# Attention of a hybrid transformer block: the order in which first-pass and second-pass score tiles take three PSUM buffers

## The chip, the cores and the metric

The kernel runs on one core of a Trainium2 chip. Its engines work side by side, each through its own instructions in order: TensorE (PE in the profile, with its weight loads as PEld), VectorE (DVE), ScalarE (ACT), GpSimd (POOL), and SyncE (SP), which issues most DMAs. The metric is the device time of one execution in microseconds; lower is better.

## The reference

The block takes x of shape (4, 1024, 256) in float32 and applies four residual steps, each on a layer-normed x: causal attention with 16 heads of 16 channels, a feed-forward step with one of four experts per token, a Mamba-2 step, and the feed-forward step again.

```python
x = x + attention(layernorm(x))   # LoRA-adapted Wq, Wk, Wv, Wo; rotary q and k
x = x + ffn(layernorm(x))         # top-1 of 4 experts, silu(x Wg) * (x Wu), then Wd
x = x + x' + mamba2(x')           # x' = layernorm(x)
x = x + ffn(layernorm(x))
```

Inside attention, which is all that this change touches:

```python
Q, K = rope(Q), rope(K)
scores = einsum('bhqd,bhkd->bhqk', Q, K) / sqrt(16)
attn = softmax(where(causal, scores, -inf))
out = einsum('bhqk,bhkd->bhqd', attn, V)
```

## The kernel before, in words

The program is laid out by a framework that tracks tiles: a Python program traces instructions in some order, a scheduler orders each engine's instructions with regard to that order, and semaphores are put where an engine needs another's result or a buffer that is still in use. An engine's own order is fixed once the program is built.

Attention works on groups of four heads. There are 16 groups in all (4 batches of 4 groups), and the code calls each group a head, `heads[n]`. For one of them the softmax takes two passes over the scores, since the row maximum is needed first:

- The **first pass**, `maxima` (L723 to L742), computes scores with queries on the partitions. For a query block `qb` of 128 and a half `h` of the keys, and for each pair `p` of two heads, two matmuls fill a tile `s1` of 128 x 2 x 512 (L733; one matmul for each head `a` of the pair, on 64 rows of the array). DVE adds the causal mask on the diagonal block (L741) and reduces the row maximum (L742). There are 12 units (`first_pass`).
- `negated` (L744 to L761) turns the maxima into a row of negated maxima, `mneg`, by four transposes. It runs after unit 3 of the first pass and after its last.
- The **second pass**, `exps` (L763 to L786), computes scores with keys on the partitions. For a block of keys `kc` and a half `qt` of the queries, and for each pair `p`, four matmuls fill a tile `s2` of the same size (L771): two with k and q, two that add the negated maximum through a selection matrix. ACT exponentiates it into a tile `pe` in SBUF (L779), and POOL zeroes what is above the diagonal (L782). There are 12 units (`second_pass`), of 512, 384, 256 or 128 columns a head.
- `weigh` (L788 to L801) multiplies `pe` with v into an accumulator `acc` (L793): four matmuls, each on 32 columns of the array. Float32 operands make each of these two instructions in the profile, so a unit has eight. `weigh` of a unit is traced one unit later, through the variable `late`.

Both `s1` and `s2` come from `ps2`, one ring of three buffers of two PSUM banks each (tag "two"; FFN tiles take `gu` from the same ring). A new tile takes the buffer of the tile three places earlier in traced order, when that has been read.

The loop at L889 goes through the heads, and for each through the 12 units of the second pass. In a unit it traces, in this order: the first-pass unit of the next head (`look(after, u)`, pairs 0 and 1), the second-pass unit of this head (`H.exps`, pairs 0 and 1), the weighing of the previous unit, and a piece of the head after the next (`then.piece(u)`): in units 2, 3, 6 and 7 `project` (L653), with matmuls L660, copies on ACT (L667, L672), the rotation on POOL (L675 to L683), casts on ACT (L690) and subtractions on POOL (L693); in units 4, 5, 8 and 9 `turn` (L697), four transposes (L701) and a copy on ACT (L708). Then come pieces of other work: the loading and output projection of batches, the routing of tokens, and FFN tiles. Head 0's own first pass stands before the loop.

After attention, the FFN, the Mamba step and the second FFN follow, from about 1273 us on.

Of the kernel before, what the change touches and what calls it, by code (L numbers as in the profile page):

```python
# [64 lines left out]
def bcast(ap, axis, n):  # L65

    a = ap.unsqueeze(axis)
    shape = list(a.shape)
    shape[axis] = n
    return a.to_broadcast(shape)  # L70
# [3 lines left out]
def hybrid_block(ctx: ExitStack, tc: tile.TileContext, t, out: bass.AP):  # L74
    nc = tc.nc
# [9 lines left out]
    def ps2(name):  # L85
        return psum_now["pool"].tile([P, 2, 512], F32, tag="two", name=name, bufs=psum_now["two"])
# [415 lines left out]
    def attention(pa):  # L502
# [34 lines left out]
        sels = []  # L537
        for p in range(2):
            w = pa.tile([P, P], F32, tag="sel", name=f"sel_{p}", bufs=2)
# [3 lines left out]
            r = pa.tile([P, P], F32R, tag="sel_r", name=f"sel_r_{p}", bufs=2)  # L543
# [96 lines left out]
        class Heads:  # L640
# [79 lines left out]
                    for p in range(2):  # L720
                        self.turn(1, u - 12, p)

            def maxima(self, qb, h):  # L723

                if self.mx is None:
                    self.mx = pa.tile([P, NBLK, 4, 2], F32, tag="mx", name=f"mx_{self.name}", bufs=2)
                keys = (qb + 1) * P
                w = min(512, keys - 512 * h)
                for p in range(2):
                    sc = ps2(f"s1_{self.name}_{qb}_{h}_{p}")  # L730
                    for a in range(2):
                        r = slice(64 * a, 64 * a + 64)
                        nc.tensor.matmul(  # L733
                            sc[:, a, 0:w],
                            self.q[p, qb // 4][r, qb % 4 * P : (qb % 4 + 1) * P],
                            self.k[p, h][r, 0:w],
                            start=True,
                            stop=True,
                        )
                    if 512 * h + w == keys:  # L740
                        nc.vector.tensor_tensor(sc[:, :, w - P : w], sc[:, :, w - P : w], bcast(amats, 1, 2), ALU.add)  # L741
                    nc.vector.tensor_reduce(self.mx[:, qb, 2 * p : 2 * p + 2, h], sc[:, :, 0:w], axis=AX.X, op=ALU.max)  # L742

            def negated(self, qt):  # L744

# [14 lines left out]
                self.mneg[qt] = pa.tile([P, 512], F32R, tag="mneg", name=f"mneg_{self.name}_{qt}", bufs=3)  # L760
                nc.vector.tensor_copy(self.mneg[qt], pt)  # L761

            def exps(self, qt, kc):  # L763
                off = max(0, kc * P - qt * 512)
                pes = []
                for p in range(2):
                    sc = ps2(f"s2_{self.name}_{qt}_{kc}_{p}")
                    for part in range(2):
                        for a in range(2):
                            r = slice(64 * a, 64 * a + 64)  # L770
                            nc.tensor.matmul(  # L771
                                sc[:, a, off:512],
                                sels[p][r, :] if part else self.k[p, kc // 4][r, kc % 4 * P : (kc % 4 + 1) * P],
                                self.mneg[qt][r, off:512] if part else self.q[p, qt][r, off:512],
                                start=(part == 0),
                                stop=(part == 1),
                            )
                    pe = pa.tile([P, 2, 512], F32, tag="pe", name=f"pe_{self.name}_{qt}_{kc}_{p}", bufs=4)
                    nc.scalar.activation(pe[:, :, off:512], sc[:, :, off:512], AF.Exp, scale=1.0 / math.sqrt(DK))  # L779
                    if kc >= 4 * qt:  # L780
                        diag = pe[:, :, off : off + P]
                        nc.gpsimd.affine_select(  # L782
                            diag, diag, [[0, 2], [1, P]], ALU.is_ge, 0.0, base=0, channel_multiplier=-1
                        )
                    pes.append(pe)
                return off, pes  # L786

            def weigh(self, qt, kc, off, pes):  # L788
                nkc = 4 * (qt + 1)
# [45 lines left out]
        second_pass = [(qt, kc) for qt in range(2) for kc in range(4 * (qt + 1))]  # L835
        heads = [Heads(n) for n in range(NB * HG)]

        def look(H, u):
            qb, h = first_pass[u]
            H.maxima(qb, h)  # L840
            if (qb, h) == (3, 0):
                H.negated(0)
            if u == len(first_pass) - 1:
                H.negated(1)
# [8 lines left out]
        H, after = heads[0], heads[1]  # L853
# [20 lines left out]
        ]  # L874
        for u in range(len(first_pass)):
            beside[u]()
            look(H, u)
        one_now = ps1
        late = None
        starting, sending, tiles, n_done = iter(()), iter(()), fill(), 0  # L880
# [1 line left out]
        def stage(n_halves):  # L882

            nonlocal n_done
            n_tiles = full_tiles(n_halves * TB) - n_done
            n_done += n_tiles
            return one_by_one(n_tiles, x_mid, f"f1_{n_halves}")

        for n, H in enumerate(heads):  # L889
            after = heads[n + 1] if n + 1 < len(heads) else None  # L890
            then = heads[n + 2] if n + 2 < len(heads) else None
            for u, (qt, kc) in enumerate(second_pass):
                if after:
                    if n and u < 2:
                        after.piece(12 + u)
                    look(after, u)
                off, pes = H.exps(qt, kc)
                if late:
                    late[0].weigh(*late[1:])
                late = (H, qt, kc, off, pes)  # L900
                if then:
                    then.piece(u)
                if H.c == 0 and n and u == 3:
                    sending = finish(H.b - 1, 1)
                if H.c == HG - 1 and u == 7:
                    sending = finish(H.b, 0)
                if H.c == 1 and H.b + 1 < NB and u == 8:
                    starting = begin(H.b + 1)
                next(starting, None)
                next(sending, None)  # L910
                if u not in (2, 3, 6, 7):
                    next(tiles, None)
                if H.c == 0 and n and u == 9:
                    for _ in tiles:
                        pass
                    tiles = stage(2 * H.b)
# [359 lines left out]
    for n, H in enumerate(halves):  # L1276
        after = halves[n + 1] if n + 1 < len(halves) else None
# [90 lines left out]
```

## Time and profile before

| what | us |
| --- | --- |
| median of 3 runs | 2649.07 |
| lowest and highest of them | 2639.3, 2653.35 |
| profiled execution, its own time | 2623.66 |
| its span, first to last instruction | 2622.0 |
| PE busy | 2301.9 |
| DVE busy | 1468.6 |
| POOL busy | 841.8 |
| ACT busy | 804.6 |

The profile is one execution. A line of a group gives the line of the kernel, the engine, the operation, what it writes and reads with the shape, and the count; after the bar the busy time of the group and the mean of one instruction in ns; after the second bar the idle time of the engine ahead of these instructions and who ended most of it. A line of the waits gives who waited for whom, then the total in us, how many times, and the longest. A line of the timeline gives the start, the duration, the engine and what ran; neighbours of one kind are merged. TensorE's matmuls are pipelined and their ends are modelled, so its busy time is not a measure of work: starts are safer.

### The profile page before, as it was taken

What the parts mean: (1) busy time and instruction counts of PE and PEld (TensorE: products, weight loads), DVE (VectorE), ACT (ScalarE), POOL (GpSimd) and SP (SyncE); (2) the same over time, 40 slices, a digit from 0 to 9 for tenths busy, and PEclk for the clock granted to TensorE, in tenths of its full rate; (3) what the DMA queues carried; (4) which work ended last, traced back from release to release, by engine and by line L of the source; (5) the groups of instructions that cost most, each with busy time, mean ns of one, the idle gap of its engine ahead of it and who ended that gap; (6) DMA issues with size and microseconds to landing.
All of it is one profiled execution on the core that took longest, in us unless ns stands there. A gap on an engine that the chain in (4) does not pass through costs nothing.

```text
span 2622.0 us, 32689 instructions
## 1 busy us (share of the span) xinstructions
PE 2301.9 (88%) x11460; PEld 1557.9 (59%) x11460; DVE 1468.6 (56%) x3573; ACT 804.6 (31%) x1582; POOL 841.8 (32%) x1244
## 2 busy tenths in 40 slices
PE   6778989998998999899989978777879899898798
PEld 4434444544555555555678854544757667687687
DVE  5445456555555455554443358777778676754232
ACT  3344444344443333333211114232323222211011
POOL 3323344233342333321222215344343333331121
PEclk8689899998899999899999988787989999999899
DMA  9993012100132111312465410001131321323552
GB/s 217 185 178 80 10 33 77 49 10 7 31 110 78 65 57 36 100 65 72 143 204 173 162 41 0 9 18 44 47 113 37 133 82 60 117 71 104 204 180 66
DMA packets 151205, 227.26 MB, mean 87 GB/s; under 512 B 25595, under 2 KB 113021, under 8 KB 151041
## 3 DMA queue, kind: packets, MB, share of 16 engines
q1 hardware_dynamic: 139328, 194.25, 25.5%
q0 software_dynamic: 11392, 30.52, 3.3%
q8 instruction: 91, 1.49, 0.2%
q14 instruction: 74, 0.60, 0.1%
q10 hardware_dynamic: 320, 0.39, 0.1%
HBM read 162.52 MB, written 62.86 MB: 86 GB/s over the span
## 4 chain that ended last, share of the span: by engine, by line
PE 63%; DVE 16%; POOL 7%; ACT 5%; issue 4%; DMA 4%; SPq 1%; POOLq 0%; ACTq 0%; DVEq 0%
PE gu_f L418 19%; PE y_f L432 9%; PE acc L793 6%; PE s L771 5%; PE mo_m L1239 3%; PE s L733 3%; PE qkv L660 3%; DVE mx L742 2%; PE turn L701 2%; DVE xc_m L1066 2%; PE xbc_m L1053 2%; POOL rope L680 2%; ACT pe L779 2%; PE y_m L1216 2%; PE po L627 1%
## 5 line engine op out<-in xcount | busy, mean ns | idle before, releaser
L742 DVE TENSOR_REDUCE mx<-s 128x2 f32<-128x1024 f32 (+3 forms) x384 | 357.2, 949 | 152.9 <-PE s L733 151.1
L779 ACT ACTIVATE pe<-s 128x1024 f32<-128x1024 f32 (+3 forms) x384 | 303.7, 808 | 297.8 <-PE s L771 293.3
L418 PE MATMUL gu_f<-t_xT_f,t_Wg_f 128*128 128x256 f32 x1216 | 325.4, 388 | 16.3 <-issue 10.2
L418 PE MATMUL gu_f<-t_xT_f,t_Wu_f 128*128 128x256 f32 x1216 | 317.2, 382 | 0.0
L793 PE MATMUL acc<-pe,v 128*32 128x512 f32 (+3 forms) x1536 | 287.7, 525 | 11.6 <-POOL pe L782 8.2
L432 PE MATMUL y_f<-t_Wd_f,t_h_f 128*128 128x256 f32 x1216 | 281.5, 386 | 6.3 <-DVE state_m L1212 2.4
L418 PEld LDWEIGHTS gu_f<-t_xT_f,t_Wg_f 128*128 128x128 f32 x1216 | 229.4, 194 | 59.5 <-issue 17.6
L143 ACT ACTIVATE t_h_f<-gu_f 128x512 f32<-128x512 f32 x152 | 90.6, 596 | 566.5 <-PE gu_f L418 566.5
L432 PEld LDWEIGHTS y_f<-t_Wd_f,t_h_f 128*128 128x128 f32 x1216 | 228.6, 192 | 49.9 <-issue 9.1
L418 PEld LDWEIGHTS gu_f<-t_xT_f,t_Wu_f 128*128 128x128 f32 x1216 | 232.2, 192 | 32.6 <-issue 1.0
L771 PE MATMUL s<-qs,ks 64*128 64x512 f32 (+3 forms) x768 | 187.4, 431 | 45.6 <-DVE mx L742 23.4
L144 DVE SCALAR_TENSOR_TENSOR t_h_f<-t_h_f,gu_f 128x512 f32<-128x512 f32 x152 | 103.9, 683 | 219.4 <-ACT t_h_f L143 219.4
L782 POOL TENSOR_SCALAR_AFFINE_SELECT pe<-pe 128x256 f32<-128x256 f32 x256 | 103.8, 407 | 380.5 <-ACT pe L779 379.4
L741 DVE TENSOR_TENSOR s<-s,amats 128x256 f32<-128x256 f32 x256 | 104.4, 426 | 200.8 <-PE s L733 160.4
L771 PEld LDWEIGHTS s<-qs,ks 64*128 64x128 f32 x768 | 87.2, 195 | 157.9 <-issue 42.4
L733 PE MATMUL s<-ks,qs 64*128 64x512 f32 (+3 forms) x768 | 158.6, 430 | 11.8 <-ACT pe L779 5.3
L771 PE MATMUL s<-mneg,sel_r 64*128 64x512 f32 (+3 forms) x768 | 167.3, 379 | 0.0
L733 PEld LDWEIGHTS s<-ks,qs 64*128 64x128 f32 x768 | 74.7, 198 | 105.9 <-issue 58.6
L675 POOL TENSOR_TENSOR rope<-qk,rope 128x256 f32<-128x256 f32 x62 | 45.2, 729 | 285.0 <-ACT qk L672 285.0
L1066 DVE SCALAR_TENSOR_TENSOR xc_m<-raw_m,conv_w,xc_m 128x512 f32<-128x512 f32 x144 | 119.3, 839 | 0.4
L660 PE MATMUL qkv<-weff,xT 128*128 128x192 f32 x512 | 114.8, 367 | 4.4 <-ACT qk L672 2.2
L660 PEld LDWEIGHTS qkv<-weff,xT 128*128 128x128 f32 x512 | 90.8, 208 | 42.8 <-issue 19.4
(340 smaller groups left out, 3616.7 us busy)
## 6 DMA issues: line engine op xcount, KB each, us to landing
t_Wg_f<-in_Wg SPq DMA_DIRECT2D x38, 1024.0 KB, 7.1
t_Wu_f<-in_Wu SPq DMA_DIRECT2D x38, 1024.0 KB, 8.0
t_Wd_f<-in_Wd SPq DMA_DIRECT2D x38, 1024.0 KB, 5.9
sorted_rows<-blank SPq DMA_DIRECT2D x17, 2056.0 KB, 31.2
t_rows_f<-sorted_rows SPq DMA_DIRECT2D x22, 514.0 KB, 5.7
x<-in_x SPq DMA_DIRECT2D x8, 512.0 KB, 3.9
o<-raw SPq DMA_DIRECT2D x128, 32.0 KB, 2.0
inv<-dens SPq DMA_DIRECT2D x128, 32.0 KB, 2.0
```

What stands on the lines that cost most here:

```text
L144: nc.vector.scalar_tensor_tensor(dst, t, 1.0, src, op0=ALU.add, op1=ALU.mult)
L418: nc.tensor.matmul(gu[:, i, j, :], w[which][:, k, f * P : (f + 1) * P], xT[:, k, :], start=(k == 0), stop=(k == 1))
L432: nc.tensor.matmul(y, hs[f // 2][:, f % 2, i * P : (i + 1) * P], wd[:, f, :], start=(f == 0), stop=(f == DFF // P - 1),)
L660: nc.tensor.matmul(pp[:, i, 0:192], B.xT[:, k, tok], B.weff[:, k, self.c * 192 : (self.c + 1) * 192], start=(k == 0), stop=(k == 1),)
L733: nc.tensor.matmul(sc[:, a, 0:w], self.q[p, qb // 4][r, qb % 4 * P : (qb % 4 + 1) * P], self.k[p, h][r, 0:w], start=True, stop=True,)
L741: nc.vector.tensor_tensor(sc[:, :, w - P : w], sc[:, :, w - P : w], bcast(amats, 1, 2), ALU.add)
L742: nc.vector.tensor_reduce(self.mx[:, qb, 2 * p : 2 * p + 2, h], sc[:, :, 0:w], axis=AX.X, op=ALU.max)
L771: nc.tensor.matmul(sc[:, a, off:512], sels[p][r, :] if part else self.k[p, kc // 4][r, kc % 4 * P : (kc % 4 + 1) * P], self.mneg[qt][r, of ...
L779: nc.scalar.activation(pe[:, :, off:512], sc[:, :, off:512], AF.Exp, scale=1.0 / math.sqrt(DK))
L782: nc.gpsimd.affine_select(diag, diag, [[0, 2], [1, P]], ALU.is_ge, 0.0, base=0, channel_multiplier=-1)
L793: nc.tensor.matmul(self.acc[32 * j : 32 * j + 32, off:512], self.v[:, kc, (DK + 1) * j : (DK + 1) * j + 32], pes[j // 2][:, j % 2, off:512 ...
L1066: nc.vector.scalar_tensor_tensor(acc, raw[:, k : k + TB], conv_w[:, cc, k : k + 1], acc, op0=ALU.mult, op1=ALU.add)
```

## The change

`maxima` and `exps` take the pair `p` as an argument and handle one pair instead of looping over both; `look` passes it on and ends early for pair 0. The loop traces, for each pair, the second-pass tile of this head and then the first-pass tile of the next one. `after.piece(12 + u)` stays ahead of them and `weigh` behind them. The same instructions are issued.

```diff
-            def maxima(self, qb, h):
+            def maxima(self, qb, h, p):
...
-                for p in range(2):
-                    sc = ps2(f"s1_{self.name}_{qb}_{h}_{p}")
...
+                sc = ps2(f"s1_{self.name}_{qb}_{h}_{p}")
...
-            def exps(self, qt, kc):
+            def exps(self, qt, kc, p):
                 off = max(0, kc * P - qt * 512)
-                pes = []
-                for p in range(2):
-                    sc = ps2(f"s2_{self.name}_{qt}_{kc}_{p}")
...
+                sc = ps2(f"s2_{self.name}_{qt}_{kc}_{p}")
...
-                return off, pes
+                return off, pe
...
-        def look(H, u):
+        def look(H, u, p):
             qb, h = first_pass[u]
-            H.maxima(qb, h)
+            H.maxima(qb, h, p)
+            if p == 0:
+                return
             if (qb, h) == (3, 0):
                 H.negated(0)
...
             beside[u]()
-            look(H, u)
+            for p in range(2):
+                look(H, u, p)
...
             for u, (qt, kc) in enumerate(second_pass):
-                if after:
-                    if n and u < 2:
-                        after.piece(12 + u)
-                    look(after, u)
-                off, pes = H.exps(qt, kc)
+                if after and n and u < 2:
+                    after.piece(12 + u)
+
+                pes = []
+                for p in range(2):
+                    off, pe = H.exps(qt, kc, p)
+                    pes.append(pe)
+                    if after:
+                        look(after, u, p)
                 if late:
                     late[0].weigh(*late[1:])
                 late = (H, qt, kc, off, pes)
```

More of the change, by code (lines that the diff above doesn't have):

```diff
@@ L728, in maxima @@
                 w = min(512, keys - 512 * h)
-                for p in range(2):
-                    sc = ps2(f"s1_{self.name}_{qb}_{h}_{p}")
[L731 to L742, printed above, removed]
+                sc = ps2(f"s1_{self.name}_{qb}_{h}_{p}")
+                for a in range(2):
+                    r = slice(64 * a, 64 * a + 64)
+                    nc.tensor.matmul(
+                        sc[:, a, 0:w],
+                        self.q[p, qb // 4][r, qb % 4 * P : (qb % 4 + 1) * P],
+                        self.k[p, h][r, 0:w],
+                        start=True,
+                        stop=True,
+                    )
+                if 512 * h + w == keys:
+                    nc.vector.tensor_tensor(sc[:, :, w - P : w], sc[:, :, w - P : w], bcast(amats, 1, 2), ALU.add)
+                nc.vector.tensor_reduce(self.mx[:, qb, 2 * p : 2 * p + 2, h], sc[:, :, 0:w], axis=AX.X, op=ALU.max)
             def negated(self, qt):
@@ L761, in negated @@
                 nc.vector.tensor_copy(self.mneg[qt], pt)
-            def exps(self, qt, kc):
+            def exps(self, qt, kc, p):
                 off = max(0, kc * P - qt * 512)
-                pes = []
-                for p in range(2):
-                    sc = ps2(f"s2_{self.name}_{qt}_{kc}_{p}")
[L768 to L783, printed above, removed]
-                        )
-                    pes.append(pe)
-                return off, pes
@@ new lines, in exps @@
+                sc = ps2(f"s2_{self.name}_{qt}_{kc}_{p}")
+                for part in range(2):
+                    for a in range(2):
+                        r = slice(64 * a, 64 * a + 64)
+                        nc.tensor.matmul(
+                            sc[:, a, off:512],
+                            sels[p][r, :] if part else self.k[p, kc // 4][r, kc % 4 * P : (kc % 4 + 1) * P],
+                            self.mneg[qt][r, off:512] if part else self.q[p, qt][r, off:512],
+                            start=(part == 0),
+                            stop=(part == 1),
+                        )
@@ L788, in weigh @@
+                pe = pa.tile([P, 2, 512], F32, tag="pe", name=f"pe_{self.name}_{qt}_{kc}_{p}", bufs=4)
+                nc.scalar.activation(pe[:, :, off:512], sc[:, :, off:512], AF.Exp, scale=1.0 / math.sqrt(DK))
+                if kc >= 4 * qt:
+                    diag = pe[:, :, off : off + P]
+                    nc.gpsimd.affine_select(diag, diag, [[0, 2], [1, P]], ALU.is_ge, 0.0, base=0, channel_multiplier=-1)
+                return off, pe
             def weigh(self, qt, kc, off, pes):
```

## The prediction

> **What bounds the kernel now.** I read the page first, then the table of windows for the attention stretch (first to last second-pass matmul, 84 to 1273 us), then the waits of TensorE in that stretch, then the timeline of one unit. From the page:
>
> ```profile
> span 2622.0 us, 32689 instructions
> PE 2301.9 (88%) x11460; PEld 1557.9 (59%) x11460; DVE 1468.6 (56%) x3573; ACT 804.6 (31%) x1582; POOL 841.8 (32%) x1244
> L742 DVE TENSOR_REDUCE mx<-s 128x2 f32<-128x1024 f32 (+3 forms) x384 | 357.2, 949 | 152.9 <-PE s L733 151.1
> L779 ACT ACTIVATE pe<-s 128x1024 f32<-128x1024 f32 (+3 forms) x384 | 303.7, 808 | 297.8 <-PE s L771 293.3
> L793 PE MATMUL acc<-pe,v 128*32 128x512 f32 (+3 forms) x1536 | 287.7, 525 | 11.6 <-POOL pe L782 8.2
> ```
>
> TensorE is the busiest engine, and the two engines that empty the score banks wait for it (the last column). The windows say the same of the attention stretch:
>
> ```profile
> 84.00:1273.00 1189.00, 1075.12 (x6016) 596.05 (x6016) 626.56 (x1465) 488.49 (x934) 391.73 (x767) 0.93 0.26 68
> ```
>
> The columns are length, then busy time of PE, PEld, DVE, ACT and POOL. DVE is busy 53% of this stretch and ACT 41%, so neither is full; PE is idle for 1189 - 1075 = 114 us. Who ends that idle time (total, times, longest):
>
> ```profile
> PE turn L701 <- POOL qtok L693: 25.3, 14, 2.3
> PE s L771 <- DVE mx L742: 23.4, 30, 5.1
> PE s L771 <- ACT pe L779: 17.8, 15, 3.0
> PE acc L793 <- POOL pe L782: 8.2, 5, 2.8
> PE s L733 <- ACT pe L779: 5.3, 13, 1.4
> ```
>
> The second, third and fifth rows, 46.5 us, are waits for one of the three score buffers. The first row is another chain: the turns wait for the rotated q that POOL makes. Busy time hides a further loss, seen in the timeline of one unit (start, duration):
>
> ```profile
> 546.60 0.74 PE L733 MATMUL s<-ks,qs 64*128 64x512 f32 x4
> 547.14 2.35 DVE L742 TENSOR_REDUCE mx<-s 128x2 f32<-128x1024 f32 x2 [5.32 <-PE s L733]
> ...
> 547.73 1.05 PE L793 MATMUL acc<-pe,v 128*32 128x512 f32 x2
> 547.89 1.02 ACT L779 ACTIVATE pe<-s 128x1024 f32<-128x1024 f32 x1 [0.61 <-PE s L771]
> 548.70 0.19 PEld L771 LDWEIGHTS s<-qs,ks 64*128 64x128 f32 x2 [0.84 <-DVE mx L742]
> 548.70 0.50 PE L771 MATMUL s<-qs,ks 64*128 64x512 f32 x2
> ...
> 549.37 1.06 PE L793 MATMUL acc<-pe,v 128*32 128x512 f32 x6
> ```
>
> Two first-pass tiles are filled, then one second-pass tile; the next needs the buffer that DVE is still reducing. A quarter of the weighing (2 of 8 acc matmuls) was ordered into that hole, and the other 6 follow later. Both pieces last about 1 us: 0.97 us from start to start for 2, and the whole of 8 also takes 0.99 us where it is not cut. A cut weighing costs a second full pass.
>
> **What the Trainium skill says.** "TensorEngine Tiling (Array Packing)", Key Properties, says that changing the tiling mode drains TensorE. The trace agrees: two passes of L660 step 0.325 us when another L660 follows and 0.418 when a row-tiled score matmul does, 0.093 us for a change. "TensorE: Matmul & The Clock Gate", The mechanism, says that tiles in different column groups run together, which is why 2 and 8 acc matmuls last alike. "PSUM — Partial Sum Buffer", Engine vs sequencer instructions, says that matmuls start in program order: a score matmul that waits for a bank holds everything behind it, as at 548.70.
>
> **The change part by part.** No instruction is added, removed or resized, and no DMA moves. Call a first-pass tile A and a second-pass tile B. Before, the ring of three buffers is taken A0 A1 B0 B1; after, B0 A0 B1 A1. Head 0's own first pass before the loop, and the last head, which has no A beside it, keep their order.
>
> *Which waits go and come.* Each tile waits for the release three places earlier. Before: B1 waits for this unit's A0 (DVE), the other three for tiles of the unit before. After: A1 waits for this unit's B0 (ACT), B0 and B1 for the previous A0 and A1 (DVE), A0 for the previous B1 (ACT). So in each unit one near wait is exchanged for another. The exponential is the shorter one: 1.02 us at full width, against 1.2 for a reduce with a mask addition of 0.43 ahead of it in 8 of 12 units; and between B0 and A1 lie A0 and a larger B1 (0.23 + 0.46 us) where A1 and B0 lay before.
>
> *TensorE's own work.* The two programs' instruction orders, as built, differ more than the diff tells, since a scheduler places the independent work. Counting unbroken pieces of weighing by width, 512 / 384 / 256 / 128 columns: 161, 56, 54, 52 before, and 159, 47, 46, 37 after. At 0.98, 0.77, 0.58 and 0.36 us a piece (start to start in the trace) that is 2.0 + 6.9 + 4.6 + 5.4 = 19 us less. Changes of tiling mode from the first B to the last acc go from 1130 to 990: 140 x 0.093 = 13 us less. Row pairs of B cut apart rise by 12, at some 0.2 us: 2 us more. Sum: 30 us less work.
>
> *One unit by hand*, from the durations above, with a projection (L660, 1.3 us) and full width: B0 starts at 0, its exponential runs from 0.73 to 1.75 as in the timeline; A0 and B1 are done at 1.15; A1 starts at 1.85, 0.7 us idle; then weighing 1.0, projection 1.3 and three changes of mode, and the next B0 starts at 4.65. Before, the timeline has successive units of this kind at 546.60, 551.85 and 556.98: 5.2 us. With a turn (0.66 us) instead of a projection it comes to 4.0, and to 4.3 if B0's exponential is 0.3 us late behind ACT's casts; the trace has 4.76 to the next unit (561.74). So a full-width unit gains about 0.5 us. Narrow units have shorter drains and shorter pieces: half of that.
>
> *The sum.* 15 heads x 12 units have both passes, half of them near full width: 90 x 0.5 + 90 x 0.25 = 67 us. That is an upper value, because heads that carry FFN tiles, or the ends and starts of batches, have other work to cover waits; there only the 30 us of work counts. I take the middle, 48 us, less the turn rows: PE reaches a turn some 0.2 us earlier against the same POOL chain, 14 times, 3 us back. **Forecast: 45 us less.** The profiled execution took 2623.7 us outside and 2622.0 as span, so it would take 2579; the median of the three timed runs is 25 us above it, and 2649 - 45 = 2604.
>
> *What is costed at nothing.* `negated` now follows the second A behind a B1: its result is used by the next head, for half 0 eight units later and for half 1 four units later; without that cover, its chain would cost the 1 us or so of four transposes and a copy, 32 times. Mask and reduce of one tile now follow each other on DVE where two additions stood together; DVE is idle 47% of the stretch. Weighing comes behind A1 and so may start later, but the weighed tiles are a unit old. On ACT, exponentials now stand between the q/k copy and the casts that wait for POOL's rotation in 41 of 64 projections, 18 before; ACT waits 2.3 us there (125.0 us in 54 waits). That unblocks a release; its own worth lies between 0 and 23 us (23 exponentials a microsecond earlier), and the unit's sum holds it.
>
> **The rivals.** *The rotation takes over.* The turns behind a projection wait for a chain of copy, POOL's three operations (2.4 us), cast and subtraction; if PE saves its time just ahead of them, the first waits row grows from 25 to some 55 us and the 30 us of work come back. For it: that row is the largest, and two projections precede the turn by one and two narrow units. Against: only one place in a head. It leaves about 10 us: 2639.
>
> *Slower: A1 is left bare.* The same-unit wait on ACT has only A0 and B1 as cover, and ACT is in order: an exponential behind casts that wait for POOL can be late by 2.3 us. If the bare wait averages 0.6 us in all 180 units, it costs 108 us; against it stand 30 us of work and the 46.5 us of buffer waits removed. 108 - 77 = 31 us slower, 2680. It decides from 77 / 180 = 0.43 us a unit. My own 0.7 at full width lies above that, which is why this is a serious rival; against it, narrow units need only 0.3, and in 86 places a quarter of the weighing still stands as cover.
>
> *The change does not do what it says*, because the scheduler regroups the tiles: runs of A and of B alternate 722 times in the new order and 360 in the old, so this is out.
>
> **How the numbers follow.** Forecast case (gain of 20 to 90 us) 0.68; rotation takes over 0.15; A1 bare 0.13; something larger than all this, 0.04. The range of the first case is 2560 to 2630; to leave out no more than 2 in 10 it reaches through the second case into the third: 2556 to 2660. A measurement of this kernel tells about 0.5% (13 us) from no change: faster by more 0.70, within 0.14, slower by more 0.16.
>
> **What would show it.** In the new profile, PE's waits on DVE's reduce should fall under 12 us and its score waits should be on ACT, at the first pass line. The attention stretch should end near 1225 to 1235 us instead of 1273, the rest staying at 1349. Acc matmuls should come mostly in eights. If PE's first-pass matmuls wait over 70 us on ACT the slower rival holds; if the turns wait over 45 us on POOL, the rotation does.

## The result and the profile after

The changed kernel takes **2632.32 us** (median of 13 runs, 2624.56 to 2637.86) where the kernel before takes 2649.07 on the same chip (13 runs, 2634.64 to 2659.13). The ratio is 0.9937, 95% interval 0.9919 to 0.9955: 17 us less. On two other chips it was 0.9942 (0.9924 to 0.9960) and 0.9962 (0.9946 to 0.9978), or 17 and 11 us less. The forecast was 45 us less.

One caution for all that follows: a profile is one execution, and chips differ. Before takes 2644 to 2652 us on the chips on which after was profiled, and its own profiles are of executions of 2620 to 2624 us. The difference of two spans is therefore not the worth of the change. After's profiled execution took 2637.86 us, its slowest of 13.

From the page of after:

```profile
span 2636.2 us, 32669 instructions
PE 2291.9 (87%) x11460; PEld 1562.9 (59%) x11460; DVE 1484.2 (56%) x3573; ACT 809.2 (31%) x1582; POOL 842.6 (32%) x1244
L741 DVE TENSOR_REDUCE mx<-s 128x2 f32<-128x1024 f32 (+3 forms) x384 | 364.1, 954 | 105.5 <-PE s L732 98.9
L776 ACT ACTIVATE pe<-s 128x1024 f32<-128x1024 f32 (+3 forms) x384 | 307.7, 810 | 320.6 <-PE s L768 290.4
```

(L741, L776 and L787 are the L742, L779 and L793 of before; L732 and L768 are its L733 and L771.) The same instructions take about the same time, and the two engines that empty the banks still wait for TensorE. TensorE's waits in the attention stretch of after (total, times, longest), however, are not what was forecast:

```profile
PE s L732 <- ACT pe L776: 27.6, 42, 2.1
PE turn L701 <- POOL qtok L693: 25.7, 15, 2.3
PE s L768 <- DVE mx L741: 15.7, 10, 10.1
PE s L768 <- ACT pe L776: 15.0, 12, 2.4
PE s L732 <- DVE mx L741: 12.0, 9, 7.0
```

The first-pass row on ACT, 5.3 us before, is now the largest. Counted tile by tile, 24.4 of its 27.6 us stand before A1: it is the new near wait on B0. The rows on DVE's reduce did not fall. They were 24.2 us in 33 waits before (23.4, and 0.8 at the first pass, a row that the prediction's list does not reach), 18 to 19 us in two further profiles of before, and are 27.7 in 19 now. Two single waits of 10.1 and 7.0 us make the most of it; the others come to 10.6 us. All waits for a score buffer together grew from 47.3 to 70.3 us. The turns stayed at 25 us.

The unit itself runs as the prediction worked it out. TensorE's timeline of after:

```profile
553.80 0.41 PE L768 MATMUL s<-qs,ks 64*128 64x512 f32 x2
...
554.92 0.50 PE L732 MATMUL s<-ks,qs 64*128 64x512 f32 x2 [0.48 <-ACT pe L776]
555.35 1.06 PE L787 MATMUL acc<-pe,v 128*32 128x512 f32 x8
556.35 1.57 PE L660 MATMUL qkv<-weff,xT 128*128 128x192 f32 x8
```

B1 is filled, A1 waits 0.48 us bare, and the weighing is whole: 1.06 us for eight, where before 2 and 6 cost that each. Successive units begin at 553.01, 557.85, 562.57, 566.49 and 570.95: 4.84 and 4.72 us with a projection (by hand 4.65, before 5.2), 3.92 and 4.46 with a turn (by hand 4.0 to 4.3, before 4.76 and 5.50).

**Which buffer a tile really takes.** The text ahead of the prediction says that a tile takes the buffer of the tile three places earlier in traced order. In the programs as built that holds for many tiles, not for all: the framework also hands out buffers in another order. Of the 180 units with both passes, B1 takes A0's buffer in 132 in before, and that of its own B0 in 23. In after, A1 takes B0's in 126, and B1 takes its own B0's in 50. So before has near waits on ACT too. The timeline of before at unit 3 of head 3, ACT and TensorE:

```profile
305.26 0.37 ACT L779 ACTIVATE pe<-s 128x256 f32<-128x256 f32 x1
305.69 0.33 PE L771 MATMUL s<-qs,ks 64*128 64x128 f32 x2 [2.98 <-ACT pe L779]
```

B1 starts when the exponential of its own B0 is done, and that one stands behind the casts that wait for POOL's rotation. Heads 0, 1, 3 and 7 have such a wait of 3.0 us in each of before's three profiles; they are 11.9 of the 17.8 us of the prediction's third row. With each of them comes a stretch of 7 to 20 us at half clock. This is head 3's (columns as in the prediction; the third from last is the clock, 1 for full):

```profile
307.00:324.10 17.10, 16.18 (x58) 8.25 (x54) 5.78 (x12) 5.92 (x11) 4.38 (x9) 0.50 0.07 17
```

In after that wait is gone; in heads 0, 3 and 7 B0 of the next unit waits 2.4 us instead, with 0 to 7 us at half clock.

**An account of the stretch.** The clock in the traces has only two values, full and half, in stretches of about 3.4 us and its multiples. The Trainium skill says so too ("TensorE: Matmul & The Clock Gate", What's actually happening). From each trace I sum, from the first second-pass matmul to the last acc, TensorE's idle time ahead of matmuls (pauses over 60 ns) and the time at half clock. What is left of the length after idle time and half of the half-clock time is called work:

| kernel | length | idle | half clock | work |
| --- | --- | --- | --- | --- |
| before, three profiles | 1190 to 1194 | 105 to 113 | 158 to 186 | 995 to 999 |
| after, three profiles | 1199 to 1213 | 132 to 142 | 216 to 236 | 953 to 957 |

By the means of three, work fell by 41 us and idle time rose by 28. Idle time that lies within half-clock stretches (13 us in before, 19 to 27 in after) is taken off one and a half times here; taken off once, work is 1002 to 1005 us before and 966 to 967 after, which is 37 us less. Half-clock time is 53 us longer too, but this column holds the chips' and executions' own spread.

About half of the added idle time lies in the first 146 us of the stretch (from 84 to 230 us: 18 to 25 us of it in before, 33 to 36 in after), where the DMA engines are busiest (0.85 to 0.96 of the time from 84 to 220 us).

### The profile page after: what moved, and what is told of

Its sections match the earlier page's. It is cut to its first block, busy times and chain, and to the rows that moved or that the text cites. A ratio compares the mean times of both kernels' runs of the same rounds, so it can differ in the third digit from the quotient of the medians.

```text
span 2636.2 us, 32669 instructions
## 1 busy us (share of the span) xinstructions
PE 2291.9 (87%) x11460; PEld 1562.9 (59%) x11460; DVE 1484.2 (56%) x3573; ACT 809.2 (31%) x1582; POOL 842.6 (32%) x1244
## 4 chain that ended last, share of the span: by engine, by line
PE 62%; DVE 15%; POOL 6%; ACT 6%; DMA 5%; issue 4%; SPq 1%; POOLq 0%; ACTq 0%; DVEq 0%
PE gu_f L418 18%; PE y_f L432 8%; PE acc L787 7%; PE s L768 5%; PE s L732 3%; PE mo_m L1240 3%; PE turn L701 3%; PE qkv L660 3%; DVE xc_m L1067 2%; PE xbc_m L1054 2%; PE y_m L1217 2%; DVE mx L741 2%; ACT pe L776 2%; POOL rope L680 2%; POOL rope L675 1%
## 5 line engine op out<-in xcount | busy, mean ns | idle before, releaser
L741 DVE TENSOR_REDUCE mx<-s 128x2 f32<-128x1024 f32 (+3 forms) x384 | 364.1, 954 | 105.5 <-PE s L732 98.9
L776 ACT ACTIVATE pe<-s 128x1024 f32<-128x1024 f32 (+3 forms) x384 | 307.7, 810 | 320.6 <-PE s L768 290.4
L787 PE MATMUL acc<-pe,v 128*32 128x512 f32 (+3 forms) x1536 | 281.4, 546 | 5.4 <-POOL pe L779 3.1
L432 PE MATMUL y_f<-t_Wd_f,t_h_f 128*128 128x256 f32 x1216 | 276.2, 382 | 7.2 <-DVE state_m L1213 2.4
L779 POOL TENSOR_SCALAR_AFFINE_SELECT pe<-pe 128x256 f32<-128x256 f32 x256 | 104.6, 411 | 415.9 <-ACT pe L776 415.0
L768 PE MATMUL s<-qs,ks 64*128 64x512 f32 (+3 forms) x768 | 193.7, 448 | 39.7 <-DVE mx L741 15.7
L732 PE MATMUL s<-ks,qs 64*128 64x512 f32 (+3 forms) x768 | 186.4, 425 | 44.6 <-ACT pe L776 27.6
L768 PEld LDWEIGHTS s<-qs,ks 64*128 64x128 f32 x768 | 87.7, 200 | 170.1 <-issue 77.5
L768 PE MATMUL s<-mneg,sel_r 64*128 64x512 f32 (+3 forms) x768 | 172.5, 384 | 0.0
L732 PEld LDWEIGHTS s<-ks,qs 64*128 64x128 f32 x768 | 94.3, 209 | 105.6 <-ACT pe L776 52.1
L660 PE MATMUL qkv<-weff,xT 128*128 128x192 f32 x512 | 108.6, 358 | 8.0 <-DVE mneg L760 4.4
```

The source lines that it names most:

```text
L432: nc.tensor.matmul(y, hs[f // 2][:, f % 2, i * P : (i + 1) * P], wd[:, f, :], start=(f == 0), stop=(f == DFF // P - 1),)
L660: nc.tensor.matmul(pp[:, i, 0:192], B.xT[:, k, tok], B.weff[:, k, self.c * 192 : (self.c + 1) * 192], start=(k == 0), stop=(k == 1),)
L732: nc.tensor.matmul(sc[:, a, 0:w], self.q[p, qb // 4][r, qb % 4 * P : (qb % 4 + 1) * P], self.k[p, h][r, 0:w], start=True, stop=True,)
L768: nc.tensor.matmul(sc[:, a, off:512], sels[p][r, :] if part else self.k[p, kc // 4][r, kc % 4 * P : (kc % 4 + 1) * P], self.mneg[qt][r, of ...
L779: nc.gpsimd.affine_select(diag, diag, [[0, 2], [1, P]], ALU.is_ge, 0.0, base=0, channel_multiplier=-1)
L787: nc.tensor.matmul(self.acc[32 * j : 32 * j + 32, off:512], self.v[:, kc, (DK + 1) * j : (DK + 1) * j + 32], pes[j // 2][:, j % 2, off:512 ...
```

## The experiments

Where an order is called pinned, the matmuls of scores and weighing in the loop got order-only dependencies, so that the scheduler keeps them on TensorE as the loop traces them:

```diff
+        def pin(made):
+            ...
+            if pinned["last"] is not None:
+                tc.add_manual_dep(made.ins, pinned["last"].ins.name, ...)   # order only, no semaphore
+            pinned["last"] = made
...
-                    nc.tensor.matmul(
+                    pin(nc.tensor.matmul(
...
-                for p in range(2):
-                    off, pe = H.exps(qt, kc, p)
-                    ...
+                for what in ('B0', 'A0', 'B1', 'A1', 'W'):
```

The experiments then differ in that one tuple. Line numbers of the pinned kernels are 13 above after's (L745, L754, L781, L789 for first pass, reduce, second pass, exponential).

**1. The order alone, with no cut allowed as cover.** `pin_pairs` is A0 A1 B0 B1 W, `pin_alt` is B0 A0 B1 A1 W.

> The old order A0 A1 B0 B1, with the weighing kept whole behind B1: score and weighing matmuls of the loop may not pass each other on TensorE. Counted in the built order, weighing comes in 117, 37, 34, 39 pieces of 512, 384, 256, 128 columns, against 161, 56, 54, 52 in the kernel before, and the tiling mode changes 977 times against 1130: by the prediction's prices 74 + 14 = 88 us less work. If such work is simply paid (the prediction's step), the time falls to some 2560 us. If a cut piece of weighing only stood in a wait that was there anyway (the theory of cover), the time stays within 12 us of before and TensorE's waits on DVE's reduce rise from 24 us to over 70. If long waits halve the granted clock (the theory of the clock), it is slower than before, with a lower mean clock in the attention stretch.

> The new order B0 A0 B1 A1 with the weighing kept whole behind A1. Pieces of weighing 125, 38, 33, 39 against 159, 47, 46, 37 in the changed kernel, 943 changes of mode against 990: 47 + 4 = 51 us less work. Paid work: 2581 us. Cover: within 10 us of the changed kernel's 2632, and first-pass waits on ACT up from 27.6 us to 50 or more. Clock: as cover or slower, mean clock of the attention stretch under 0.90.

Measured on one chip: `pin_pairs` 2667.1 us, ratio to before 1.0112 (1.0090 to 1.0134); `pin_alt` 2616.9, 0.9916 (0.9899 to 0.9932). TensorE's waits of `pin_pairs`:

```profile
PE s L781 <- ACT pe L789: 44.0, 36, 3.5
PE s L781 <- DVE mx L754: 28.8, 43, 1.9
PE s L745 <- DVE mx L754: 17.6, 8, 7.1
```

and of `pin_alt`:

```profile
PE s L745 <- ACT pe L789: 44.3, 54, 3.3
PE s L781 <- DVE mx L754: 18.7, 18, 6.3
PE s L781 <- ACT pe L789: 15.3, 16, 2.6
```

Their work is alike (907 and 917 us); idle time is 178 against 149 and half-clock time 301 against 243. So with the same work the order of the tiles is worth 50 us, all of it in idle time and in the clock. Of the cases expected of `pin_pairs`, that of the clock came: it is slower than before, with a mean clock over its runs of 0.892 where before has 0.910. The sign of the theory of cover, over 70 us of waits on DVE's reduce, did not: they are 46.4. For `pin_alt` cover came nearest: by its ratio it is 6 us below after, with the first pass's waits on ACT up from 27.6 to 44.3 us (50 were expected).

Nor is the loss of `pin_pairs` all at the near wait on DVE. Its largest row holds 33.6 us of B1 on ACT, of which 23.3 us are seven waits at unit 3 like the one shown for before: there too B1 has the buffer of its own B0, in 36 of 180 units. The timeline of `pin_pairs` at a unit 11 shows it:

```profile
147.97 2.35 DVE L754 TENSOR_REDUCE mx<-s 128x2 f32<-128x1024 f32 x2
148.04 0.33 PE L781 MATMUL s<-qs,ks 64*128 64x128 f32 x2 [0.54 <-ACT pe L789]
```

B1 starts at 148.04, when the reduce of A0, the first of the two, has only begun.

Before is 1.1% better than the pinned pairs, so the scheduler's free order, which cuts weighings into 323 pieces where `pin_pairs` has 227, had already taken half of what the new order could bring. After, left free, is no better than `pin_alt`.

**2. Which part of the order counts.** `pin_bpairs` is B0 B1 A0 A1 W (near wait on ACT, tiles in pairs), `pin_afirst` is A0 B0 A1 B1 W (alternating, near wait on DVE).

> Order B0 B1 A0 A1 W, pinned as in the first four runs: grouped like the old order, but the wait inside the unit is that of A1 for B0's exponential, on ACT. Its work is that of B0 A0 B1 A1 W within 5 us (pieces of weighing 123, 37, 34, 33). If it matters which engine drains the buffer of the wait inside the unit, it is within 12 us of that kernel (2617 us). If it matters that tiles of the two kinds alternate, so that neither DVE nor ACT gets two in a row, it is within 12 us of A0 A1 B0 B1 W (2667 us).

> Order A0 B0 A1 B1 W, pinned: alternating, but the wait inside the unit is that of B1 for A0's reduce, on DVE. The opposite of the run before: near 2617 us if alternating matters, near 2667 us if the engine of the near wait does.

Measured: `pin_bpairs` 2615.9 us, 0.9955 (0.9940 to 0.9971); `pin_afirst` 2630.9, 1.0003 (0.9986 to 1.0020). Four orders make a square:

| | near wait on DVE | near wait on ACT |
| --- | --- | --- |
| in pairs | 1.0112 | 0.9955 |
| alternating | 1.0003 | 0.9916 |

Each half gains by itself, and least where the other is already there. Giving the near wait to ACT is worth more (1.6% and 0.9%) than alternating (1.1% and 0.4%). Each row and column is from two chips, so 0.3% says nothing here. The headings hold for most units only: as built, B1 is near its own B0 in 78 of 180 units of `pin_afirst`. And what they gain is not always waits. In pairs, idle time falls from 178 to 141 us with the near wait on ACT. In alternation it rises, from 131 to 149, at like work (920 and 917 us), while half-clock time falls from 292 to 243 and the mean clock of the runs rises from 0.894 to 0.9025: that 0.9% lies in the clock, and why is not shown.

**3. Cover for the near wait.** `pin_alt_cover` puts the whole weighing ahead of A1, `pin_pairs_cover` (A0 A1 B0 W B1) ahead of B1, and `pin_alt_cut` a quarter of it:

```diff
-                for what in ('B0', 'A0', 'B1', 'A1', 'W'):
+                for what in ('B0', 'A0', 'B1', 'W0', 'A1', 'W'):   # W0: head 0 of the four, W: the other three
```

> The new order with the whole weighing between B1 and A1, where it covers the exponential of B0 that A1 waits for. Pieces 123, 37, 34, 34, 992 changes of mode: about 52 us less work than the changed kernel. Paid work alone: 2580 us. Cover: the bare wait of A1 (27.6 us of idle) goes and no piece is cut, so 2590 to 2605, first-pass waits on ACT under 12 us. Clock: more than the waits themselves, since the clock stays up: under 2590 with a mean clock over 0.93 in the attention stretch.

> The old order with the whole weighing between B0 and B1, where it covers the reduce of A0 that B1 waits for. Pieces 127, 36, 35, 35, 986 changes of mode. If what matters is that the near wait is covered, and not which engine it is on, it lies within 10 us of the kernel B0 A0 B1 weigh A1. If alternating by itself is worth the forecast 45 us, it is 30 us or more slower than that one. Paid work alone: 66 + 13 us less than before, 2570.

> Order B0 A0 B1 w A1 W, pinned, where w is a quarter of the weighing (one of its four column groups) and W the other three: every weighing is cut, and the piece stands in A1's wait for ACT. Against the uncut kernel (2617 us, 149 us idle in the attention stretch, 243 us of it at half clock) the prices say 111 us more for pieces and 27 for changes of mode. Paid work: 2755 us. If a piece in a wait is free and also keeps the clock up: first-pass waits on ACT fall from 45 to under 12 us, the time at half clock to under 170 us, and the time is 2640 to 2690 us.

Measured: 2621.2 us, 0.9925 (0.9909 to 0.9942); 2671.4 us, 1.0100 (1.0067 to 1.0133); 2668.3 us, 1.0160 (1.0118 to 1.0201). The whole weighing takes the waits of the first pass on ACT from 44.3 to 12.5 us, but those of the second pass on ACT rise from 15.3 to 28.2 and those of the first pass on DVE from 5.5 to 15.6, and nothing is gained. Nor does the whole weighing help the pairs (1.0100 against 1.0112), though it fills their waits: idle time falls from 178 to 139 us, but half-clock time rises from 301 to 363 and work by 20. So with both near waits filled the two orders still differ by 50 us, at the same idle time (140 and 139 us): half-clock time is 93 us longer in the old order, and work 14. The near wait is then not all that the order decides. (A quarter of the weighing in the hole of the old order, as before has it, was not tried with that order pinned.) In the new order the cut shows what a piece really costs. TensorE's waits of `pin_alt_cut` at the first pass on ACT:

```profile
PE s L745 <- ACT pe L789: 11.5, 12, 2.4
```

As built it has 380 pieces of weighing, `pin_alt` 235. Its work is 126 us more, 0.87 us a piece with the added changes of tiling mode in it: a second pass is paid in full. But its idle time is 110 us instead of 149 and its half-clock time 157 instead of 243, so that the stretch is only 45 us longer: two thirds of the price come back as less idle time and a fuller clock, as was expected for a piece in a wait. (By the two ratios, from two chips, it is 64 us longer and half comes back.) The prediction had counted the removal of such pieces as work saved and the waits as saved besides.

**4. The casts ahead of the exponential.** `pin_alt_casts` is `pin_alt` with the q and k casts on POOL, so that no exponential stands behind an ACT that waits for POOL's rotation:

```diff
-                        nc.scalar.copy(wn[:, n].bitcast(F32R), bcast(r[:, n], 2, 2))
+                        by.tensor_copy(wn[:, n].bitcast(F32R), bcast(r[:, n], 2, 2))
```

> B0 A0 B1 A1 W pinned (0.9916 of before), with the casts of q and k that wait for POOL's rotation moved from ACT to POOL, so that no exponential stands behind such a wait in ACT's queue. If the first pass waits on ACT because the exponentials stand behind those casts (125 us of ACT idle in the kernel before), TensorE's score waits on ACT fall from 61 us to under 35 and the time by 10 to 25 us, though turns may wait longer for the busier POOL (27 us now, up to 40). If it is only the exponential's own 1 us behind B0, they stay within 10 us of 61.

Measured: 2607.6 us, 0.9877 (0.9808 to 0.9945). Its waits:

```profile
PE turn L714 <- POOL qtok L706: 33.0, 16, 3.5
PE s L745 <- ACT pe L789: 19.1, 37, 1.5
PE s L781 <- ACT pe L789: 3.6, 9, 1.1
```

The score waits on ACT fall from 59.6 to 22.7 us (A1's own from 42.0 to 18.7), and the turns' wait on POOL rises from 26.8 to 33.0. So more than half of the bare A1 was the exponential's delay behind the casts, as the prediction's slower rival feared. In time it is worth 10 us by the two ratios, which is not clear of their intervals: idle time falls by 20 us, but half-clock time rises by 58.

**5. DVE behind a DMA.** The waits of 10.1 and 7.0 us in after look alike. The timeline of after, DVE and TensorE at the first:

```profile
132.48 0.25 DVE L814 RECIPROCAL den<-den 128x16 f32<-128x16 f32 x1 [17.14 <-DMA den<-raw]
132.65 1.16 DVE L741 TENSOR_REDUCE mx<-s 128x2 f32<-128x1024 f32 x1
133.86 0.80 PE L768 MATMUL s<-qs,ks 64*128 64x512 f32 x2 [10.06 <-DVE mx L741]
```

DVE stands 17 us at the reciprocal of `divide`, whose operand a DMA still brings; the reduce behind it, and with it the buffer, wait too. "TensorE: Matmul & The Clock Gate", Architectural detail, says that DVE is strictly first in, first out, which these lines bear out. (The second wait is like it: DVE stands 5.5 us at `layernorm`, behind the load of x.) `after_late` traces both later, `alt_casts_late` does so on `pin_alt_casts`:

```diff
-                nc.vector.reciprocal(den, den)
-                ...
+                def rest():                      # reciprocal and all behind it
+                    nc.vector.reciprocal(den, den)
+                    ...
+                owed.append([2, rest])           # two units later
...
-                if b == 0:
-                    yield
+                yield                            # layernorm a unit after the load
```

> Kernel after with two DVE steps that stand behind a DMA moved later in traced order: the second half of divide (reciprocal of den and all that follows) two units later, and layernorm in begin one unit after the load of x. No work is added. Theory that DVE, in order, holds the score buffers while it waits for a DMA in the first 230 us: the waits of PE on DVE above 5 us there (10.1, 7.0 and 3.7 us in after, 9.5, 6.1 and 6.0 in its second profile) go, PE's idle time in the attention stretch falls from 132 to 110-120 us, the half-clock time that follows them by 10 to 30 us more, 10 to 30 us less in all: 2597-2617 where after takes 2627. Rival that these long waits are only where a delay shows that something else would cause: the idle time comes back as waits on ACT or on the matmuls' own inputs, within 5 us of after.

> The fastest kernel so far (turns in alternation pinned, casts on POOL: 2608 us against a before of 2644) with the same two DVE steps moved later. Its own longest wait on DVE in that stretch is only 5.0 us, so if the waits behind DMAs are what this edit removes, it gains less here than in after: 0 to 10 us, 2598-2608 on a before of 2644, and the waits on POOL at the turns (33.8 us) stay. Rival that the edit helps in other ways (a shorter queue on SP): as much as in after, 10 to 30 us.

Measured: `after_late` 2608.4 us, 0.9955 (0.9939 to 0.9970), on a chip where before takes 2622.8, so no better by its ratio than after elsewhere; in its profile idle time is 120 us but work 970, since the scheduler cut more weighings again (95 pieces of two where after has 86). `alt_casts_late` 2586.0 us, 0.9857 (0.9841 to 0.9873): the fastest of all, 37 us below before, and as expected little more than `pin_alt_casts`. Its idle time is the same as there (130 us). To judge the edit beside after itself, both ran on one more chip (`same_after`, `same_late`).

> Kernel after, unchanged, on the same chip as the two edits of it below. Its ratio to before was 0.9937 and 0.9942 on two chips where before took 2649 and 2644 us. If the gain depends on the chip through before's own clock (0.9096 where before took 2644, 0.9146 where it took 2623 to 2627), it is smaller on a chip where before is fast: 0.997-1.0 there; if not, 0.993-0.995 everywhere.

> after_late again beside after on one chip. If the long waits of PE on a DVE that stands behind a DMA cost what they last, it takes 8 to 20 us less than after beside it (idle time 12 us less in its profile, half-clock time shorter too, work 13 us more); rival: the scheduler's other order of the weighing takes it back, within 5 us of after.

Measured: after 2641.6 us, 0.9962, which fits neither expected case, since before is no quick one on this chip; with the edit 2632.4, 0.9937 (0.9916 to 0.9958); before 2652.4. The edit's 9 us lie at the low end of what was expected, and the two intervals overlap. The profile tells why it is no clean test: there the operand comes so late that two units are not enough. From the waits of DVE and of TensorE in `same_late`:

```profile
DVE den L824 <- DMA den<-raw: 36.4, 8, 22.8
PE s L777 <- DVE mx L750: 23.6, 13, 17.3
```

That DVE behind a DMA holds a score buffer is shown by the lines; that it costs after some 10 us is likely and not settled.

**6. The clock in a batch's first head.** Heads 4 and 8, where the last batch's output projection and routing run beside attention, are longer in after. The windows of head 4 (columns as in the prediction), of before:

```profile
356.30:431.50 75.20, 68.59 (x384) 36.58 (x386) 45.42 (x148) 35.79 (x72) 28.16 (x53) 0.95 0.10 29
```

and of after, with a part of it:

```profile
346.31:432.31 86.00, 79.84 (x386) 39.88 (x382) 47.23 (x137) 35.75 (x71) 28.23 (x54) 0.79 0.10 26
351.00:368.00 17.00, 16.65 (x56) 7.10 (x58) 7.63 (x15) 5.76 (x11) 2.04 (x5) 0.51 0.09 16
```

Eleven us more at the same idle time: the clock falls from 0.95 to 0.79. For 17 us TensorE is busy 98% of the time at half clock, behind waits of 0.65 and 1.08 us and in the course of a third of 0.39, all within 5 us. The timeline there shows that this is no slip of the clock record:

```profile
351.86 1.92 PE L787 MATMUL acc<-pe,v 128*32 128x512 f32 x2
353.71 0.69 PE L768 MATMUL s<-qs,ks 64*128 64x384 f32 x2
```

From the start of the piece to the next start are 1.85 us, where it is 0.98 at full clock.

Heads 4 and 8 together hold 71 to 76 us at half clock in after's three profiles and 31, 31 and 44 in before's. `after_early` and `before_early` move only the batch's work by one unit:

```diff
-                if H.c == 0 and n and u == 3:
+                if H.c == 0 and n and u == 2:
                     sending = finish(H.b - 1, 1)
```

> Kernel after with one number changed: at a batch's first head, finish of the batch before starts at unit 2 instead of 3 (output projection, routing and their layer norm come one unit earlier; pieces of weighing by the built order 281 instead of 289). In after, heads 4 and 8 hold 30 and 13 us more time at half clock than in before, in both profiles, with no more idle time; that is 15 + 7 us of the 28 us by which the forecast was too high. Theory that this is a matter of where short waits of PE (0.65, 1.08, 0.39 us within 5 us at head 4) fall: with the batch's work moved a unit, the half-clock time of heads 4 and 8 (76 us in after) falls to 30-50 us and the time by 10 to 22 us: 2605-2617 where after takes 2627. Rival that the half clock there belongs to the alternation itself: heads 4 and 8 stay above 65 us, and the time within 5 us of after.

> Kernel before with the same one number changed (pieces of weighing 327 instead of 323). Heads 4 and 8 of before hold 31 us at half clock. If the placing of waits decides, this can move either way: 20 to 60 us, and the time by -5 to +15 us. If the half clock belongs to the alternation, heads 4 and 8 stay at 25-40 us and the time within 5 us of before.

Measured on one chip: 2618.9 us, 0.9971 (0.9957 to 0.9984), and 2620.5 us, 0.9982 (0.9969 to 0.9995). Half-clock time of the two heads is 57 us and 21 us: neither after's 71 to 76 nor before's 31 to 44. So the place of the other work seems to bear on it, and yet the alternation still has the more; each is one profile. Beside after on one chip:

> after_early again beside after on one chip. If the shorter half-clock time of heads 4 and 8 in its profile (57 us for 76) is more than one execution's luck, it takes 5 to 12 us less than after beside it; rival: within 4 us of it.

Measured: 2639.4 us, 0.9946 (0.9920 to 0.9972), 2 us below after. Heads 4 and 8 became 17 us shorter than in after beside it (158 for 175), but heads 5 and 9 ten us longer (173 for 163): most of the loss moved on to the next head. So the rival holds for the time, and this half clock could not be removed by moving the batch's work.

These two do give a pair of profiles from one chip, differing in the change alone: from `before_early` to `after_early` work falls from 1000 to 956 us, idle time rises from 100 to 132, half-clock time from 189 to 195. That is 43 - 32 - 3 = 8 us less. The medians show 2 us less (2620.5 to 2618.9): on this chip, with this edit in both, the change is hardly worth anything.

**7. The unchanged kernels again**, for the spread.

> The kernel before, unchanged, for a second profile. Its first profiled execution (2623.7 us) was faster than all its timed runs. The account length of the attention stretch = full-speed work + idle + half of the time at half clock fits the first six profiles; if it holds, a slower execution of the same program has the same work (about 1000 us) and idle time (within 8 us of 113), and more time at half clock than 158 us, 190 to 230.

> The changed kernel, unchanged, for a second profile: its first profiled execution (2637.9 us) was the slowest of its 13 runs, that of before the fastest. By the account (length of the attention stretch = full-speed work + idle + half of the time at half clock) it has again 956 us of work within 8, about 130 us idle, and a time at half clock below the first one's 229 us if that was an unlucky execution: 190 to 220, so that the stretch is 1180 to 1195 us long. If it has 229 or more again, the clock isn't what sets its executions apart.

> Kernel before, unchanged, for a profile on another chip. Both profiles of before so far are from executions of 2620 and 2624 us, the three of after from chips where before takes 2644 to 2652. If this chip is one of those: work of the attention stretch 994-1000 us as before (the order is fixed), idle time 105-120 us, and half-clock time higher than 158-186 us, near 200-220, which would put the change's clock loss at 10-30 us of half-clock time, not at 45. If the chip is a quick one, idle and half-clock time as in the two profiles so far.

Measured: before against itself 0.9998 and 0.9996, after 2626.5 us and 0.9942 (before 2643.9). Work and idle time came as expected in all three (995 and 106 us, 957 and 134, 996 and 105). Half-clock time was 186 us in `before_again`, under the 190 expected of a slower execution, which at 2620 us it wasn't; 216 in `after_again`, as expected, in a stretch of 1199 us, a little over the 1195. Within 47 runs of before on one chip, time falls by some 19 us for each 0.01 of mean clock (correlation -0.87). Both chips of before's new profiles were quick ones (2627 and 2620 us), so the third did not settle the clock column of the account above. What can be said of the clock comes from the runs: on the chip of `after_again` the mean was 0.9096 for before and 0.9083 for after, on that of `same_after` 0.9096 and 0.9057, and in `before_early` and `after_early` 0.9134 and 0.9107. At 19 us for 0.01 that is an estimated 2, 7 and 5 us against the change.

## Why the prediction was off

**Direction and bound: right.** TensorE sets the time of the stretch, the change moves only waits and pieces on it, and the rest of the kernel stayed: 1349 us after attention, as forecast.

**Work: right in kind, somewhat small.** 30 us forecast from pieces and mode changes; the account shows 37 to 41.

**The unit by hand: right for this head.** 4.65 and 4.0 to 4.3 us worked out, 4.84, 4.72, 3.92 and 4.46 traced. All of head 6, which these units belong to and whose half-clock time is the same before and after (10 us), became 3.0 us shorter, where 12 units at 0.375 would be 4.5.

**The sum: this step failed.** It took 0.5 and 0.25 us for all 180 units and the middle of 67 and 30. That is 18 us of waits saved beyond the work. In their place idle time grew by 28 us (32 in the pair of one chip). The four heads with little else in them (1, 3, 6 and 7) did gain 17 us, where 48 x 0.375 = 18 of the upper value of 67 were counted (means of three profiles of before and of after: 276 to 259 us), but that agreement is luck. By the account they have 11 us less work, 7 more idle time, and 27 less at half clock, which is 14: what went is mostly the slow stretch beside the 3.0 us waits of heads 1, 3 and 7, which the prediction did not count. The other eleven, counted on for 49, did not gain at all in these profiles. They are 30 us longer: 30 less work, 20 more idle time, and 80 more at half clock, a part of which is the chips'. Four reasons for the idle time were found:

- The pieces counted as waste were cover as well. Pinned, the new order is worth 50 us; free, 11 to 17, because before's free order had taken 1.1% off the pinned pairs already, and in the pinned new order a piece in a wait gives back half to two thirds of its price (experiments 1 and 3). The step "one near wait is exchanged for another" compared two bare waits, while in the timeline of before one of them has a piece in it. That this piece alone makes the 1.1% is argued, not shown.
- The new near wait is on an in-order ACT, and it came to 27.6 us in 42 waits where 5.3 stood before. In the pinned order more than half of such waits are the casts' delay (experiment 4), which the prediction knew and left inside the unit's sum.
- "PE's waits on DVE's reduce should fall under 12 us" failed, 27.7 us: without two waits it would be 10.6, so the far wait on DVE is seldom late by the reduce itself, but DVE can stand 17 us behind a DMA (experiment 5).
- "Each tile waits for the release three places earlier" is not what was built: 23 of 180 units of before had B1 near ACT already, and 50 of after still have it.

**What was not priced: the clock.** The prediction took TensorE's times as fixed. The trace of before showed 0.93 in the windows and was read past. Half-clock stretches of 3 to 14 us stand beside most of the waits over 2 us in after's first profile. But idle time alone does not set them: `pin_pairs_cover` has 39 us less of it than `pin_pairs` and 62 us more at half clock, and `pin_alt` and `pin_alt_cover` beat their like (`pin_afirst`, `pin_pairs_cover`) by the clock and not by idle time. Over all profiles half-clock time goes with the number of pieces that weighings are cut into: 157 us at 380 pieces, 158 to 189 at 323 to 327, 168 to 236 at 281 to 298, and 231 to 363 at 219 to 235. No experiment separates the pieces from the waits they fill. By the runs' mean clock the change lost an estimated 2 to 7 us by it; how much of the profiles' longer half-clock time belongs to the change, and what sets that clock, stays open.

**The rivals.** The rotation did not take over: 25.7 us at the turns, far from 45. A1 was not the 108 us of the slower rival: 27.6 us against the 70 from which it would have decided. But its mechanism gave 22 us of added waits, the largest single part. Whole weighings did become more frequent, 107 as built against 64, but not nearly all of 192. The stretch did not end at 1225 to 1235 us but at 1287 in the profiled execution.

11 to 17 us less against 45 is then, in round terms: 37 to 41 of work, less 28 of idle time, less 2 to 7 of clock. That leaves 2 to 11, so some 5 to 10 us of what the runs say are not accounted for.

## What to carry to other kernels

A busy piece of work in a hole may be the hole's cover: before counting it as saved, ask what wait stands there without it, and price the two together. In a ring of buffers look for the nearest release, in the program as built and not as traced: here it was worth 0.9 to 1.6%, a part of it through the clock, to have it on the engine with the shorter reading. Look at what is queued ahead of that reading too, DMAs included. What a scheduler may rearrange has to be compared with the order pinned and free; here the free one had taken half of the gain already. And a gain that matches its sum may still come from elsewhere: take the clock out first.

## What the runs showed of the hardware

- TensorE ran 17 us at half clock while it was busy 98% of the time. In the 3.4 us before, it was idle for 1.4 us in all and 1.08 at most at a time. "TensorE: Matmul & The Clock Gate", What's actually happening, has the half clock come after an idle window of about 3.4 us and go after a busy one of that length; here neither holds, and the start-to-start time of a piece (1.85 us for 0.98) bears the clock record out.
- The DMAs that bring `den`, 8 KB in all, kept DVE waiting for 17.1 us in one execution and 22.8 in another. Both waits lie in the first 220 us, where the DMA engines are busy all but throughout (0.96 and 0.95 from 84 to 220 us). A part of the wait is SyncE's: in after it issued the four from 111.9 to 125.2 us.
